# Expert layer of a four-layer conv mixer: when the group sums run, how block sums and weight sums are cut, and where filler matmuls stand

## The chip, the cores and the metric

The kernel runs on one core of one Trainium2 chip. The metric is the device time of one execution in microseconds (us). Five engines work side by side, each with its own queue of instructions in order: TensorE (PE; matmuls, with PEld for its weight loads), VectorE (DVE), ScalarE (ACT), GpSimd (POOL) and SyncE (SP, which issues DMAs). An engine waits for another through semaphores only.

## The reference, cut to what matters

Input x has 8 images of 384 channels and 32x32 pixels, in float32. Four layers follow each other, each as x = x + layer(group_norm(x)), with 32 groups of 12 channels. The change is in layer 1, the experts:

```
x = x + L1(gn(x)):   scores -> top 2 of 4 experts per token
  present[k, e] = any token of the whole batch has e as its k-th choice
  h_e = relu(x . w1_e + b1_e);  y_e = h_e . w2_e + b2_e       (384 -> 384 -> 384)
  out = sum_e y_e * coef_e,  coef_e = sum_k present[k, e] * w_k
```

Where every expert is chosen by some token in both places, all coefficients are one, and the layer is the plain sum of the four experts' outputs. The kernel computes that, keeps the logits, and decides later whether a second pass by token is needed; on these inputs it is not. Behind the layer, group norm needs mean and variance over 12 channels and all pixels of an image.

## The kernel before, in words

Channels lie on partitions, 384 as three tiles (`NC = 3`) of 128. `experts()` (from L1140) loops over the 8 images b and over two halves h of each, 512 pixels a half, cut again into two quarters of 256 columns (`QF`). There are 16 rounds, called here first half and second half of an image. A round has two phases.

*Hidden phase.* For experts 0 to 2 the product w1 . x is made by a fast scheme with 15 block products instead of 18. `dual` (L1284) issues one matmul of 128x256 per product (two records each in the profile) on sums of input blocks, the "forms" (`make_forms`, L1273, 12 sums on GpSimd, a round ahead), and on sums of w1's blocks (`w1sum`, made once by `sum_weights`, L1259). VectorE combines the 15 results out of PSUM (L1304), ScalarE adds bias and rectifies (L1282). The last expert goes the plain way (`classical`, L1310): 3 output tiles by 3 input tiles, nine matmuls of 128x512. These nine are dealt out as fillers, some after the second product of each of the experts 0, 1 and 2 and the rest at the end (L1460 to L1472). In the first round of all, every expert goes the plain way.

*Product phase.* `products` (L1339) multiplies by w2 with the same scheme transposed: 15 products, each of four matmuls of 128x256 (one per expert, eight records), into one PSUM buffer out of five. VectorE adds each result to one to four blocks of the residual r (L1353, L1355). The operands are blocks of the hidden values hs or sums of them, `hs_sum`: eight sums (`HSUMS[:-2]`) before the phase, by GpSimd for each expert as it is ready, and two sums over all experts (128x1024) issued after product 8. Products 0 to 4 read plain blocks; products 5 to 12 read the eight sums in turn, products 13 and 14 the last two. In first halves from image 1 on GpSimd makes those two, else VectorE.

After product i a round runs the jobs listed for i. In first halves from image 1 on these include the steps of `next_layer` (L1383) for the image before: moments of its three channel tiles (`moments2`, L1366, with `centred`, L309, three small VectorE instructions), the sums over groups (`over_groups`, L300, 14 small matmul records into `gn_ps`), `norm2` (L1377, four small VectorE instructions, a power on GpSimd at L332 and a VectorE instruction at L337 which reads it), and four steps that normalise (ScalarE), transpose (VectorE) and store a tile. Other jobs normalise the image's second half, make its forms and fetch the next image's residual. In second halves VectorE adds the layer input to the next image's residual (L1164).

The order of every engine but SP here is the order in which the program writes the instructions (`manual_schedule`). An engine that waits holds up all that is queued behind.

Of the kernel before, what the change touches and what calls it, by code (L numbers as in the profile page):

```python
# [21 lines left out]
NC = C // P  # L22
# [8 lines left out]
E, HID = 4, 384  # L31
# [33 lines left out]
def taps(xp, dy, dx, rows=H, h0=0):  # L65
# [20 lines left out]
WSUMS = (  # L86
    (7, (2, 0), -1, (2, 2)),
    (6, 7, 1, (0, 0)),
    (7, 7, -1, (1, 0)),
    (2, (1, 1), -1, (1, 2)),  # L90
    (3, 2, 1, (0, 1)),
    (2, 2, -1, (2, 1)),
    (10, 6, 1, 3),
    (10, 10, -1, (0, 2)),
# [6 lines left out]
HSUMS = (  # L101
    (4, (1, 1), (2, 1)),
    (0, (0, 1), (2, 1)),
    (10, (2, 0), (2, 1)),
    (3, (1, 1), 10),
    (8, (1, 0), 3),
    (11, (0, 0), 8),
    (6, (0, 1), 10),
    (9, (0, 0), 6),
# [5 lines left out]
R15 = 3  # L115
FORMS = (
    (4, (1, 1), (0, 1), -1),
    (14, 4, (2, 1), 1),
    (13, (2, 0), 14, -1),
    (1, (0, 0), (1, 0), -1),  # L120
    (0, (0, 0), (2, 0), -1),
    (11, (0, 1), (2, 0), -1),
    (3, (2, 1), (0, 1), -1),
    (10, (1, 0), 14, -1),
# [49 lines left out]
def conv_mixer_kernel(ctx: ExitStack, tc: tile.TileContext, a: dict, out: bass.AP):  # L174
    nc = tc.nc
# [234 lines left out]
    with (  # L410
# [38 lines left out]
        with tc.tile_pool(name="cps", bufs=2, space=PSUM, reuse_waits="tile") as cps:  # L449
# [68 lines left out]
            for n, (ct, v, u) in enumerate(groups):  # L518
                if u == 0:

                    o = co.tile([P, B, H, 32], FP, tag="o", name="o")
                w = weights0.pop(n).rearrange("p r t w -> p r (t w)")
                ps = cps.tile([P, 4, 2, B, H], FP, tag="ps", name="ps")
                for cc in range(2):
                    for k in range(3):
                        for e, d, i in product(range(2), repeat=3):
                            r = slice(64 * i, 64 * i + 64)
# [63 lines left out]
    def layers(again, early, xst, pre_pool, pp0, pw):  # L591
# [548 lines left out]
        def experts():  # L1140
# [14 lines left out]
            rs, xns, pls = {}, {}, {}  # L1155
# [97 lines left out]
            def block1(n):  # L1253
                n = {8: (1, 1), 9: (2, 0)}.get(n, n)
                if isinstance(n, tuple):
                    return w1[:, :R15, n[0], n[1] * P : (n[1] + 1) * P]
                return w1sum[:, w1slot[n]]

            def sum_weights():  # L1259
                for o, i, sign, j in [*WSUMS[3:6], *WSUMS[8:10], *WSUMS[:3], *WSUMS[6:8], *WSUMS[10:]]:  # L1260
                    first8 = o == 8 and i != 8
                    nc.gpsimd.tensor_tensor(
                        out=block1(5 if first8 else o), in0=block1(5 if i == 8 else i), in1=block1(j),
                        op=ALU.add if sign > 0 else ALU.subtract,
                    )
# [4 lines left out]
                    return xn[:, n[0], n[1] * QF : (n[1] + 1) * QF]  # L1270
                return forms[:, fslot[n]]

            def make_forms(xn, part=slice(0, len(FORMS))):  # L1273
                for o, i, j, sign in FORMS[part]:
                    i, j = (form_of(v, xn) for v in (i, j))
                    nc.gpsimd.tensor_tensor(
                        out=forms[:, fslot[o]], in0=i, in1=j,
                        op=ALU.add if sign > 0 else ALU.subtract,
                    )
# [55 lines left out]
            def sums(hs, some, s, eng=nc.vector):  # L1335
                for o, i, j in some:
                    eng.tensor_add(rows_of(o, hs, s), rows_of(i, hs, s), rows_of(j, hs, s))  # L1337
# [25 lines left out]
                    for job in jobs.get(i, ()):  # L1363
                        job()

            def moments2(r, b, cts, mv, dq):  # L1366

                for ct in cts:
                    bs = small.tile([P, 2, 6], FP, tag="gn_bs", name="gn_bs")
                    bn_stats_of(bs, r[:, ct, :])  # L1370
                    nc.vector.bn_aggr(mv[:, :, ct], bs.rearrange("p a s -> p (a s)"))
                c = slice(cts[0], cts[-1] + 1)
                centred(
                    dq[:, c], mv[:, 0, c].unsqueeze(2), mv[:, 1, c].unsqueeze(2), ref2[:, c, b : b + 1]
                )
# [7 lines left out]
            def next_layer(b):  # L1383

                r = rs[b]
                mv = small.tile([P, 2, NC], FP, tag="gn_mv", name="gn_mv")
                if b < B - 1:
                    dq = er.tile([P, NC, 2, 1], FP, tag="dq", name="dq")
                    st = er.tile([P, NC, 3], FP, tag="st", name="st")
                    keep_residual(r, b)  # L1390
                    for ct in range(NC):
                        moments2(r, b, (ct,), mv, dq)
                        yield
                    ps = eh.tile([P, NC, 2, 1], FP, tag="sm", name="gn_ps")
                    over_groups(ps, dq, range(NC))
                    yield
                    norm2(ps, b, range(NC), st)
                    yield
                    steps = pass_on_steps(r, b, st[:, :, 0], st[:, :, 1], er)
                    for _ in steps:  # L1400
                        yield
                    return
                dq = er.tile([P, NC, 2, 1], FP, tag="dq", name="dq")
                st = er.tile([P, NC, 3], FP, tag="st", name="st")
                parts = (range(2), range(2, NC))
                cos = (range(1), range(1, NC))
                for i, (cts, co) in enumerate(zip(parts, cos)):
                    if i == len(parts) - 1:
                        keep_residual(r, b)
                    moments2(r, b, cts, mv, dq)  # L1410
                    yield
                    ps = eh.tile([P, NC, 2, 1], FP, tag="sm", name="gn_ps")
                    over_groups(ps, dq, co)
                    yield
                    norm2(ps, b, co, st)
                    yield
                    for ct in co:
                        pass_on(r, b, ct, st[:, :, 0], st[:, :, 1], er)
                        yield
# [26 lines left out]
            for b, h in product(range(B), range(2)):  # L1446
                hs = ew.tile([P, NC, E, HF], FP, tag="hs", name="hs")
                xn = xns[b, h]
                gating = logits(b) if h else iter(())
                if (b, h) == (0, 0):  # L1450
                    for e in (E - 1, *range(E - 1)):
                        for _ in classical(hs, e, range(NC), xn):
                            pass
                        if e == E - 3:
                            for s in (slice(E - 1, E), slice(0, E - 2)):
                                sums(hs, HSUMS[:-2], s)
                    sums(hs, HSUMS[:-2], slice(E - 2, E - 1))
                    sum_weights()
                else:
                    full = classical(hs, E - 1, range(NC), xn)  # L1460
                    for e in range(R15):
                        got = {}
                        dual(hs, e, xn, slice(0, 2), got)
                        next(gating, None)
                        for _ in range(2):
                            next(full)
                        dual(hs, e, xn, slice(2, len(DUAL)), got)
                        if e:
                            sums(hs, HSUMS[:-2], slice(e - 1, e), nc.gpsimd)
                    next(gating, None)  # L1470
                    for _ in full:
                        pass  # L1472
                    for e in range(R15 - 1, E):
                        sums(hs, HSUMS[:-2], slice(e, e + 1), nc.gpsimd)
                if (b, h) == (B - 1, 1):
                    wqpool.close()
                    begin_layer2(B - 1, er)
                jobs = {}

                def at(i, job, *args):  # L1480
                    jobs.setdefault(i, []).append(lambda: job(*args))

                nxt = (b, 1) if h == 0 else (b + 1, 0)
                if h == 0:
                    if passing:
                        for i in (0, 1, 2, 4, 5, 7, 8, 10, 12):
                            at(i, next, passing)
                    at(2, normed, b, 1)
                    half = len(FORMS) // 2
                    at(3, lambda b=b: make_forms(xns[b, 1], slice(0, half)))  # L1490
                    at(6, lambda b=b: make_forms(xns[b, 1], slice(half, len(FORMS))))
                    if b + 1 < B:
                        at(13, fetch_next, b + 1)
                elif b + 1 < B:
                    for i in (0, 1, 3):
                        at(i, next, ahead[b + 1])
                    at(4, normed, b + 1, 0)
                    at(5, lambda b=b: make_forms(xns[b + 1, 0]))
                products(b, h, hs, jobs)
                if h == 1:  # L1500
                    passing = next_layer(b)
# [302 lines left out]
        sums = fe.tile([P, 2, B, 5], FP, name="sums")  # L1804
# [172 lines left out]
        with tc.manual_schedule(engines=ORDERED | {mybir.EngineType.Pool}):  # L1977

            for ct in range(NC):
                o = None  # L1980
                for c in range(8):
# [10 lines left out]
                    if c == 0:  # L1992
# [3 lines left out]
                        o = to.tile([P, B, H, 32], FP, tag="o", name="o")  # L1996
# [562 lines left out]
```

## Time and profile before

| What | Value |
|---|---|
| Median of 3 runs | 3197.67 us (3193.99 to 3200.61) |
| Profiled execution | 3198.98 us, span 3197.1 us |
| Busy: PE, DVE, ACT, POOL | 94%, 60%, 38%, 25% of the span |
| Experts' layer | about 1730 to 2690 us of the span |
| Two rounds (one image) in it | 119.1 to 120.1 us |
| Mean granted TensorE clock | 0.977 of full speed |

The rows that follow name a source line, an engine, the tiles written and read, the shape, a count, and in brackets the engine's idle time before and what ended it. A view by windows gives busy times in a stretch and the granted clock as a share of full speed. Times of rows count from the start of the span.

### The profile page before, as it was taken

How to read it: one execution, taken by the hardware profiler on the slowest of the kernel's cores; microseconds unless marked ns; L12 is line 12 of the kernel's file. 1: busy time of each engine (PE TensorE's matmuls, PEld its weight loads, DVE VectorE, ACT ScalarE, POOL GpSimd, SP SyncE). 2: the span in 40 equal slices, each digit the busy share in tenths (PEclk: the TensorE clock that was granted, in tenths of full speed). 3: DMA queues.
4: the chain of work that ended last, by engine and by line, in shares of the span. 5: the costliest groups of instructions: out<-in, count | busy, mean ns of one | idle time of the engine just before them, and what ended most of it. 6: DMA issues, size and time to landing. Idle time of an engine off the chain costs nothing.

```text
span 3197.1 us, 45217 instructions
## 1 busy us (share of the span) xinstructions
PE 3000.7 (94%) x18280; PEld 1710.7 (54%) x18280; DVE 1907.5 (60%) x3221; ACT 1212.6 (38%) x1446; POOL 807.4 (25%) x1102
## 2 busy tenths in 40 slices
PE   4988999999999999999998999999999999886999
PEld 3765334343434334343433777777777777555543
DVE  6998344444454454444445777777777776447174
ACT  3555453535444453535342122222222222446520
POOL 2432000000000000000003565665665663111400
PEclk9999999999999999999999999999999999988999
DMA  6787011020101111020013012112111114866766
GB/s 220 271 284 288 20 42 62 23 72 33 62 23 60 45 44 58 23 82 23 13 43 142 19 46 59 62 50 54 64 51 52 51 44 137 330 212 232 233 223 190
DMA packets 89107, 323.03 MB, mean 101 GB/s; under 512 B 13608, under 2 KB 16000, under 8 KB 84664
## 3 DMA queue, kind: packets, MB, share of 16 engines
q1 hardware_dynamic: 64936, 251.71, 23.4%
q10 hardware_dynamic: 13776, 35.82, 3.5%
q0 software_dynamic: 10176, 32.51, 3.0%
q8 instruction: 146, 2.39, 0.3%
q14 instruction: 73, 0.60, 0.1%
HBM read 211.66 MB, written 111.68 MB: 101 GB/s over the span
## 4 chain that ended last, share of the span: by engine, by line
PE 73%; DVE 14%; DMA 5%; POOL 3%; issue 3%; ACT 2%; SPq 0%; ACTq 0%; DVEq 0%; POOLq 0%
PE sc L771 15%; PE av L790 14%; PE p L1344 10%; PE p L1295 7%; PE sc L669 7%; PE sc L724 4%; PE ph L1314 4%; PE sc L846 4%; DVE stats L250 2%; DVE y L499 2%; POOL hs_sum L1337 2%; PE ps L1956 2%; DMA w<-in_w 1%; DVE hs L1304 1%; PE po L2370 1%
## 5 line engine op out<-in xcount | busy, mean ns | idle before, releaser
L778 ACT ACTIVATE e<-sc 128x1024 f32<-128x1024 f32 x512 | 483.1, 1029 | 608.2 <-PE sc L771 608.1
L771 PE MATMUL sc<-qT,kT 64*128 64x512 f32 x2048 | 473.9, 602 | 0.0
L790 PE MATMUL av<-e,vT 128*64 128x512 f32 x2048 | 467.7, 598 | 0.0
L771 PEld LDWEIGHTS sc<-qT,kT 64*128 64x128 f32 x2048 | 186.7, 186 | 282.1 <-issue 231.2
L790 PEld LDWEIGHTS av<-e,vT 128*64 128x64 f32 x2048 | 135.5, 136 | 316.5 <-issue 316.5
L1337 POOL TENSOR_TENSOR hs_sum<-hs,hs_sum 128x256 f32<-128x256 f32 (+1 forms) x314 | 266.7, 857 | 19.4
L820 POOL DMA_DIRECT2D att<-att x45 | 23.8, 531 | 979.9 <-DVE att L815 979.9
L806 DVE LOAD_MASK_SELECT sm<-av x64 | 0.9, 14 | 417.0 <-PE av L790 417.0
L669 PE MATMUL sc<-y,pw 128*128 128x512 f32 x576 | 249.3, 594 | 0.0
L528 PE MATMUL ps<-xt,wx 64*64 64x256 f32 x3456 | 196.9, 386 | 36.7 <-DVE xt L466 21.4
L1353 DVE TENSOR_TENSOR r<-r,p 128x256 f32<-128x256 f32 x416 | 154.6, 413 | 106.8 <-PE p L1344 105.2
L808 DVE RECIPROCAL inv<-sm 128x512 f32<-128x512 f32 x64 | 214.6, 3353 | 2.2
L352 ACT ACTIVATE hs<-hs,b 128x512 f32<-128x512 f32 x135 | 89.1, 715 | 322.8 <-DVE hs L1304 322.8
L1337 POOL TENSOR_TENSOR hs_sum<-hs 128x256 f32<-128x256 f32 x180 | 132.8, 766 | 293.0 <-ACT hs L352 293.0
L528 PEld LDWEIGHTS ps<-xt,wx 64*64 64x64 f32 x3456 | 156.3, 137 | 76.2 <-issue 38.3
L669 PEld LDWEIGHTS sc<-y,pw 128*128 128x128 f32 x576 | 108.8, 190 | 140.0 <-issue 138.6
L1114 PE MATMUL ps<-xt,wx 64*64 64x256 f32 (+1 forms) x2912 | 159.1, 377 | 25.4 <-ACT wx L1712 14.4
L1295 PE MATMUL p<-forms,w 128*128 128x256 f32 x630 | 174.5, 387 | 7.4 <-DVE hs_sum L1304 6.6
L1344 PE MATMUL p<-hs_sum,wsum 128*128 128x256 f32 x768 | 173.6, 379 | 0.0
L1304 DVE TENSOR_TENSOR hs<-p,hs_sum 128x256 f32<-128x256 f32 x270 | 113.6, 421 | 83.3 <-PE p L1295 35.6
L1314 PE MATMUL ph<-xn,w 128*128 128x512 f32 x342 | 159.5, 601 | 3.0 <-ACT xn L352 3.0
L1344 PEld LDWEIGHTS p<-hs_sum,wsum 128*128 128x128 f32 x768 | 145.9, 190 | 19.8
(346 smaller groups left out, 4644.4 us busy)
## 6 DMA issues: line engine op xcount, KB each, us to landing
raw<-y SPq DMA_DIRECT2D x72, 512.0 KB
y<-raw SPq DMA_DIRECT2D x24, 1536.0 KB
x<-x SPq DMA_DIRECT2D x23, 608.0 KB
xt<-x SPq DMA_DIRECT2D x23, 608.0 KB
w<-in_w ACTq DMA_DIRECT2D x36, 384.0 KB
xn<-in_x SPq DMA_DIRECT2D x24, 512.0 KB
x<-in_x SPq DMA_DIRECT2D x16, 768.0 KB
z<-z POOLq DMA_DIRECT2D x16, 768.0 KB, 4.3
```

Source lines behind the costliest of these rows:

```text
L528: nc.tensor.matmul(ps[64 * d : 64 * d + 64, 2 * i + e, cc], lhsT=w[r, 12 * cc + 6 * e + 3 * d + k, :], rhs=xt0s[ct][r, 16 * d + 4 * u + 2 ...
L669: nc.tensor.matmul(ps[:, h, :], lhsT=w[:, ct, pair, :], rhs=y[:, ct, h * HF : (h + 1) * HF], start=ct == 0, stop=ct == NC - 1,)
L771: nc.tensor.matmul(sc[:, s, :], lhsT=kTs[b][r, pair, m * P : (m + 1) * P], rhs=qTs[b][r, pair, h * HF : (h + 1) * HF], start=True, stop=True,)
L778: nc.scalar.activation(e, sc, AF.Exp, scale=1.0 if shifted else HD**-0.5)
L790: nc.tensor.matmul(av[64 * s : 64 * s + 64, :], lhsT=vTs[0][:, m, c0 : c0 + 64], rhs=e[:, s, :], start=m == 0, stop=m == N // P - 1,)
L808: nc.vector.reciprocal(inv, sm)
L1114: nc.tensor.matmul(ps[64 * d : 64 * d + 64, 2 * i + e, c % 2, images], lhsT=w[r, d * K7 + k, :], rhs=by_slot(xts[ct])[r, 16 * d + column(c ...
L1295: nc.tensor.matmul(ps[:, :QF], lhsT=block1(PRODUCTS[n][0])[:, e], rhs=form_of(n, xn), start=True, stop=True,)
L1314: nc.tensor.matmul(ph, lhsT=w1[:, e, ct, dc * P : (dc + 1) * P], rhs=xn[:, ct, :], start=ct == 0, stop=ct == NC - 1,)
L1337: eng.tensor_add(rows_of(o, hs, s), rows_of(i, hs, s), rows_of(j, hs, s))
L1344: nc.tensor.matmul(ps[:, :QF], lhsT=block(w)[:, e], rhs=rows_of(x, hs, e), start=e == 0, stop=e == E - 1,)
L1353: nc.vector.tensor_tensor(out=o, in0=o, in1=ps[:, :QF], op=op)
```

## The change

Five edits, all in `experts()`:

1. The three centrings of an image (one per channel tile, behind each tile's moments) become one over all three tiles, as a step of its own after the moments. The group sums follow after product 6 (product 4 before), `norm2` after 7 (5), and the four passing steps after 9, 10, 12 and 14 (7, 8, 10 and 12).
2. The eight block sums of experts 2 and 3 are made together, one instruction of 512 columns for both, instead of one of 256 columns for each.
3. Of the 13 sums of w1's blocks, the first eight (in the order of the list) are issued before the first round's products, and five after product 4, behind the forms.
4. Fillers: three after the second product of expert 0, then two, two, and two at the end (before: two, two, two, three).
5. In first halves all twelve forms are issued after product 3 (before: six after 3, six after 6). The fetch of the next residual moves from product 13 to 14.

```diff
-            def sum_weights():
-                for o, i, sign, j in [*WSUMS[3:6], *WSUMS[8:10], *WSUMS[:3], *WSUMS[6:8], *WSUMS[10:]]:
+            def sum_weights(some):
+                for o, i, sign, j in some:
...
-            def moments2(r, b, cts, mv, dq):
+            def moments2(r, b, cts, mv):
...
                     nc.vector.bn_aggr(mv[:, :, ct], bs.rearrange("p a s -> p (a s)"))
+
+            def centred2(dq, mv, b, cts):
                 c = slice(cts[0], cts[-1] + 1)
                 centred(
                     dq[:, c], mv[:, 0, c].unsqueeze(2), mv[:, 1, c].unsqueeze(2), ref2[:, c, b : b + 1]
...
                     for ct in range(NC):
-                        moments2(r, b, (ct,), mv, dq)
+                        moments2(r, b, (ct,), mv)
                         yield
+                    centred2(dq, mv, b, range(NC))
+                    yield
                     ps = eh.tile([P, NC, 2, 1], FP, tag="sm", name="gn_ps")
...
-                    sum_weights()
+                    sum_weights(WSUMS[:8])
...
-                        for _ in range(2):
+                        for _ in range(2 + (e == 0)):
                             next(full)
...
-                    for e in range(R15 - 1, E):
-                        sums(hs, HSUMS[:-2], slice(e, e + 1), nc.gpsimd)
+                    sums(hs, HSUMS[:-2], slice(R15 - 1, E), nc.gpsimd)
...
                     if passing:
-                        for i in (0, 1, 2, 4, 5, 7, 8, 10, 12):
+                        for i in (0, 1, 2, 3, 6, 7, 9, 10, 12, 14):
                             at(i, next, passing)
                     at(2, normed, b, 1)
-                    half = len(FORMS) // 2
-                    at(3, lambda b=b: make_forms(xns[b, 1], slice(0, half)))
-                    at(6, lambda b=b: make_forms(xns[b, 1], slice(half, len(FORMS))))
+                    at(3, lambda b=b: make_forms(xns[b, 1]))
+                    if b == 0:
+                        at(4, sum_weights, WSUMS[8:])
                     if b + 1 < B:
-                        at(13, fetch_next, b + 1)
+                        at(14, fetch_next, b + 1)
```

More of the change, by code (lines that the diff above doesn't have):

```diff
@@ L1271, in form_of, with make_forms @@
                 return forms[:, fslot[n]]
-            def make_forms(xn, part=slice(0, len(FORMS))):
-                for o, i, j, sign in FORMS[part]:
+            def make_forms(xn):
+                for o, i, j, sign in FORMS:
                     i, j = (form_of(v, xn) for v in (i, j))
@@ L1409, in next_layer @@
                         keep_residual(r, b)
-                    moments2(r, b, cts, mv, dq)
+                    moments2(r, b, cts, mv)
+                    centred2(dq, mv, b, cts)
                     yield
```

## The prediction

> **What bounds the kernel now.** I read the engine rows of the page first, then the windows over the experts' stage (1780 to 2700 us), then TensorE's waits in it, and last the timeline of one image.
>
> ```profile
> PE 3000.7 (94%) x18280; PEld 1710.7 (54%) x18280; DVE 1907.5 (60%) x3221; ACT 1212.6 (38%) x1446; POOL 807.4 (25%) x1102
> ...
> 1840.00:1900.00 60.00, 56.17 (x233) 44.69 (x232) 44.09 (x107) 11.61 (x21) 39.59 (x53) 0.95 0.13 27
> 1900.00:1960.00 60.00, 58.28 (x265) 45.69 (x265) 46.74 (x105) 16.02 (x25) 34.75 (x44) 1.00 0.25 84
> ...
> PE gn_ps L304 <- DVE dq L313: 34.7, 16, 8.2
> PE p L1344 <- POOL hs_sum L1337: 8.7, 7, 1.3
> ```
>
> (Windows: length, then busy us and records of PE, PEld, DVE, ACT and POOL, the granted clock, DMA share, GB/s. Waits: us in total, times, longest.) TensorE sets the pace, in this stage too (56 to 58 of every 60 us). Its two stalls there are the ones the change touches: the group sums wait for VectorE's centring, and products wait for GpSimd's block sums. The window with a group sum in it has a granted clock of 0.95, the other 1.00. The timeline of image 1's first half shows why:
>
> ```profile
> 1890.39 0.28 PE L304 MATMUL gn_ps<-dq,gmatA 128*128 128x2 f32 x2
> 1891.09 0.83 PE L304 MATMUL gn_ps<-dq,gmatA 128*128 128x2 f32 x6 [0.42 <-DVE dq L313]
> 1894.86 1.44 PE L304 MATMUL gn_ps<-dq,gmatA 128*128 128x2 f32 x6 [2.94 <-DVE dq L313]
> 1896.16 5.76 PE L1344 MATMUL p<-hs_sum,w 128*128 128x256 f32 x16
> ```
>
> And three windows of 2 us across it:
>
> ```profile
> 1894.00:1896.00 2.00, 1.14 (x6) 1.14 (x6) 1.97 (x6) 0.00 (x0) 1.92 (x4) 0.50 0.00 0
> 1898.00:1900.00 2.00, 2.00 (x6) 1.63 (x5) 0.04 (x1) 0.00 (x0) 1.94 (x3) 0.50 0.00 0
> 1902.00:1904.00 2.00, 2.00 (x11) 1.77 (x10) 1.66 (x4) 1.13 (x1) 2.00 (x4) 1.00 0.00 0
> ```
>
> After the wait the clock is 0.50, and 16 matmul records take 5.76 us. At full clock 24 take 5.34, so a record is 0.2157 us and a product (8 records) 1.726. GpSimd's queue in the same half is the other thing to see:
>
> ```profile
> 1895.55 0.73 POOL L1276 TENSOR_TENSOR forms<-xn 128x256 f32<-128x256 f32 x1
> ...
> 1901.26 0.86 POOL L332 TENSOR_TENSOR st<-fm_b,mhalf 128x3 f32<-128x3 f32 x1 [1.32 <-DVE st L326]
> 1902.09 0.73 POOL L1276 TENSOR_TENSOR forms<-xn 128x256 f32<-128x256 f32 x1
> ...
> 1906.21 4.82 POOL L1337 TENSOR_TENSOR hs_sum<-hs,hs_sum 128x1024 f32<-128x1024 f32 x2
> ...
> 1902.15 0.68 DVE L337 SCALAR_TENSOR_TENSOR st<-st 128x3 f32<-128x3 f32 x1 [0.90 <-POOL st L332]
> ```
>
> Six forms, the power (L332), six forms, then two wide sums that products 13 and 14 read. It ends at 1911.0; product 13 starts only at 1912.1 (the next half at 1915.57 less two products), so GpSimd is just hidden today.
>
> **What today's stalls cost.** From the group sum's start to the next half's first matmul: 25.2, 25.0, 24.4, 25.0, 24.4, 25.0, 24.4 us for images 1 to 7, mean 24.8. Ten products are 17.26 and 14 small matmuls 0.9. So 6.6 us are lost per image, wait and slow clock together. In second halves of images 0 to 6 the first 46 records (9.92 us) start at 1945.81 and the 47th at 1957.15: 1.42 lost, 9.9 in all.
>
> **Group sums after product 6, one centring.** Now three centrings of three instructions each sit among the moments (1.3 us each: 1886.03 to 1887.37 is one). Taking them out brings the third moment's end from 1893.2 to 1890.2, with products 0.3 us earlier (below); two evictions (0.9) give 1891.1, and one centring 1.3 to 2.7 (up to two GpSimd sums of 1.27 in its way): 1892.4 to 1893.8. Product 6 ends at 1893.5. The stall goes, or 0.3 is left.
>
> **Two experts' sums together.** Per half 16 GpSimd instructions of 256 columns (0.72 us) become 8 of 512. No 512-wide sum of these blocks is in the trace. Bounds: the line through 256 columns (0.72) and 1024 (2.37) gives 1.27; w2's sums of 512 columns (L1248) run 1.27 to 1.44, the upper end beside busy VectorE. I take 1.27, since in this stretch VectorE mostly reads one operand from SBUF; 8 of them, paced as the present ones are (8 in 5.97), come to 10.4, against 11.95 now. They begin later, since the last expert's rectification (ScalarE, to 1884.13) must be done: 1884.2 to 1894.6, a gain of 0.95. The first sum is there at 1885.5, for all experts that remain, where now the last expert's is ninth. Product 5 wants it after 1891, so second halves lose their 1.42 wait: -9.9.
>
> **The forms undivided: what is late next.** All twelve now stand ahead of the power, and the wide sums behind it. Replaying image 1 on its own times: forms 1894.6 + 8.5 (4.4 + 4.1 now) = 1903.1, power to 1903.95, wide sums to 1906.35 and 1908.8. VectorE has the power's inputs by 1898.5 and then stands still, with the evictions of products 8 to 12 behind it, until its L337. That row is 0.68 now beside a form that ends with it (1902.82), 0.16 for the last image, where GpSimd is idle. So it waits for whatever GpSimd began: here a 2.4 us sum. Bounds 0.16 and 2.4; I take 2.4, as all seven images show the whole remainder waited. VectorE is free at 1906.35, product 8's bank at 1907.15. With five banks, product 13 starts then; 12 ended at 1904.8. The half ends at 1907.2 + 3.45 = 1910.65 instead of 1915.57. Group sum to end falls from 24.8 in the mean to 20.3: -4.5.
>
> The Trainium skill, page "SBUF — State Buffer", section "Who interferes with whom", says that a VectorE instruction with two SBUF inputs and a GpSimd instruction that reads SBUF exclude each other for a whole instruction. L337 (0.68 beside 0.16) agrees; by that rule the 2.4 is right, and were it 0.16 instead, the sum would be some 12 us lower.
>
> **Fillers 3, 2, 2 and 2.** One 128x512 matmul pair (0.863) moves ahead of the first expert's third product, which delays VectorE's whole chain by as much, because it waits for TensorE at each expert's start (1.2 to 2.0 us): +0.86 per first half, so -3.64 net, x7 = -25.5. At the end one filler fewer: the first product's third expert wants its rectified block 0.86 sooner (1945.81 for 1946.29), +0.53 in second halves: x8 = +4.2. In first halves it vanishes in the new wait.
>
> **Second half's start, images 1 to 7.** VectorE comes late: from 1906.35, the evictions of products 8 to 14 and three transposes (1.99 each, each behind ScalarE's 1.24) end at 1918.7, as 1906.35 + 0.75 + 0.4 + 1.4 + 2.0 + 0.75 + 0.4 + 0.1 + 2.0 + 1.4 + 1.1 + 2.0 gives. TensorE, begun at 1910.65, waits 0.65 for a bank at its second product, spends 1.4 on logits and 2.6 on three fillers, and at the eighth product waits 0.8 and a little after: +1.65, x7 = +11.6. With VectorE free 2.2 us sooner it would be 0; with GpSimd 1 us slower about 2.6.
>
> **Weights' sums in two parts.** GpSimd's total to 1780 is the same, and the next reader is at 1795. VectorE's last five sums take 0.91 beside forms, the three before 1.16 beside weights' sums; the forms now come first, so about 1.0 is gained before product 5 of image 0: -1.0. Hidden by that 15 us: the five moved sums. SP's fetch of the next residual moves one product later, behind the last read of the old one (about 1915.5 instead of 1913.5), wanted at 1948.5: nothing.
>
> **The clock.** The new gap before product 13 is 2.4 us in one piece. 2.9 after 0.4 halves the clock in all seven images, for 3.3 or 6.8 us; 1.4 in second halves never. The halving stretches begin at 3.4 us steps, and the least idle time inside such a step that halved it is 2.3 (image 3). So perhaps one image in three is hit, at 1.7 us: bounds 0 and 24 (3.4 each), taken +3. The Trainium skill, "TensorE: Matmul & The Clock Gate", section "Why this matters for your kernels", asks for no idle gap over about 3 us; by it the term is 0 and the sum 3 us lower, which no run here shows yet.
>
> Sum: -25.5 - 9.9 + 4.2 + 11.6 - 1.0 + 3 = -17.6. The profiled execution (3198.98, span 3197.1) lies 1.3 above the median of the runs, 3197.67; taken from the median: 3180.
>
> **Rivals.**
> - L337 slips in ahead of the wide sum. Product 13 then starts at 1906.4, the half ends at 1910.5, and second halves start unhindered: 3167. Against it: 0.68 in seven of seven.
> - GpSimd is no bound at all, the stalls just vanish: 46 + 10 - 8 + 1 = 49 less, 3149. It needs the queue 2.4 us shorter than any row makes it.
> - Slower: the 512-wide sums. Everything in first halves is pinned to GpSimd's queue, so each us there costs 7. Eight at 1.27 are in the sum; the gain is gone at 17.6/7/8 = 0.31 more (1.58), a clear loss from 1.7. Two present sums take 1.50 (then 3191); at 1.9 it is 3213. Against it: no 512-column row above 1.45.
> - The clock falls for 6.8 us in every image: 3201, the same within what is measurable.
> - The change doesn't do what it says: the group sums still wait at product 6. Up to 2.4 us of that would be hidden by the wait at 13; beyond, 3195.
>
> **How the numbers follow.** Chances: as summed 0.47 (own range 3170 to 3190), L337 early 0.12, no new bound 0.08, GpSimd slower 0.19, clock 0.08, group sums still waiting 0.06. About 0.2% (6.4 us) is what a measurement can tell. Faster 0.67, same 0.14, slower 0.19. Range 3154 to 3204: from near the free case to the slower case's edge.
>
> **What would show it.** Right: group sums wait under 0.5 us; no POOL wait in second halves; L337 at about 2.4 us; a gap before product 13, put down to VectorE's evictions or hs_sum; 512-wide sums at 1.27. Wrong: L337 at 0.16 or 0.7, full clock with products unbroken, or 512-wide rows over 1.5.

## The result, and the profile after

| | before | after |
|---|---|---|
| median | 3196.01 us (4 runs, 3193.99 to 3200.61) | 3170.97 us (4 runs, 3165.36 to 3177.68) |
| profiled execution | 3198.98 us, span 3197.1 | 3177.68 us, span 3175.9 |

The ratio of the times is 0.9921, with a 95% interval of 0.9896 to 0.9945: faster by 0.8%, or 25 us between the medians. The profiled execution of after is the slowest of its four, so that the two profiles lie only 21.3 us apart. The time forecast was 3180.

The page's row of engines and the two windows that were shown of before, now of after (in the second kind of line: length, busy us and records of PE, PEld, DVE, ACT and POOL, granted clock, DMA share, GB/s):

```profile
PE 3001.4 (95%) x18280; PEld 1696.7 (53%) x18280; DVE 1912.0 (60%) x3179; ACT 1213.5 (38%) x1446; POOL 787.4 (25%) x982
```
```profile
1840.00:1900.00 60.00, 59.11 (x259) 47.31 (x258) 45.18 (x109) 11.76 (x21) 39.29 (x46) 1.00 0.15 32
1900.00:1960.00 60.00, 57.63 (x257) 43.07 (x256) 47.84 (x99) 15.97 (x25) 35.96 (x40) 1.00 0.25 84
```

TensorE's records are as many as before. VectorE has 42 fewer (14 centrings of three instructions each), GpSimd 120 fewer (15 rounds of eight sums each). The window with image 1's group sums went from 56.17 to 59.11 us of busy TensorE, and from a clock of 0.95 to 1.00. The next window lost: 58.28 to 57.63. Both matter below.

TensorE's waits from 1720 to 2700 us of after, which is the experts' layer and a little on both sides (total us, times, longest):

```profile
PE gn_ps L304 <- DVE dq L313: 11.1, 2, 8.2
PE p L1344 <- DVE r L1353: 8.7, 7, 1.3
...
PE p L1344 <- ACT hs L352: 6.2, 15, 0.4
```

The group sums' wait for the centring fell from 34.7 us in 16 places to 11.1 in two, and those two lie outside the seven first halves. The wait for `hs_sum` (8.7 us in seven) is gone. A new one stands in their place, again seven times, 1.3 us at most: product 13 waits for an eviction (L1353). And the first product of 15 rounds waits 0.4 us for ScalarE's rectification.

Image 1's first half in after, TensorE:

```profile
1883.11 4.58 PE L1344 MATMUL p<-hs,w 128*128 128x256 f32 x20 [0.42 <-ACT hs L352]
...
1894.43 1.62 PE L304 MATMUL gn_ps<-dq,gmatA 128*128 128x2 f32 x14
1895.91 5.43 PE L1344 MATMUL p<-hs_sum,wsum 128*128 128x256 f32 x24
...
1902.90 3.62 PE L1344 MATMUL p<-hs_sum,wsum 128*128 128x256 f32 x16
1907.78 1.97 PE L1344 MATMUL p<-hs_sum,w 128*128 128x256 f32 x8 [1.26 <-DVE r L1353]
```

GpSimd and VectorE in the same stretch:

```profile
1884.98 3.75 POOL L1337 TENSOR_TENSOR hs_sum<-hs 128x512 f32<-128x512 f32 x3 [3.82 <-ACT hs L1324]
1888.81 6.54 POOL L1337 TENSOR_TENSOR hs_sum<-hs,hs_sum 128x512 f32<-128x512 f32 x5
1895.31 0.72 POOL L1276 TENSOR_TENSOR forms<-xn 128x256 f32<-128x256 f32 x1
...
1903.77 0.86 POOL L332 TENSOR_TENSOR st<-fm_b,mhalf 128x3 f32<-128x3 f32 x1
1904.60 4.80 POOL L1337 TENSOR_TENSOR hs_sum<-hs,hs_sum 128x1024 f32<-128x1024 f32 x2
```
```profile
1904.67 2.30 DVE L337 SCALAR_TENSOR_TENSOR st<-st 128x3 f32<-128x3 f32 x1 [4.95 <-POOL st L332]
1906.89 2.59 DVE L1353 TENSOR_TENSOR r<-r,p 128x256 f32<-128x256 f32 x7
...
1916.83 1.98 DVE L1014 STREAM_TRANSPOSE x<-xn 128x1024 f32<-128x1024 f32 x1
```

Read it as a relay. GpSimd works without a break from 1884.98 to 1909.40: sums, twelve forms, the power, the wide sums. VectorE idles 4.95 us until the power is there, and its answer, L337, works on three columns but takes 2.30 us; GpSimd's first wide sum starts 0.07 us ahead of it, and `last_dve` below shows that this is the reason. Seven evictions wait behind L337, and product 13 waits for the first two of them, which are product 8's, because products 8 to 12 hold all five banks.

To compare whole images, I cut the layer at the first matmul record of each phase (L1295 or L1314 for a hidden phase, L1344 for a product phase). The layer runs here from the first matmul of image 0 to the first matmul of the next layer.

| mean us | before | after |
|---|---|---|
| image 0, first half: hidden phase | 32.81 | 33.21 |
| image 0, first half: product phase | 33.22 | 30.48 |
| first halves, images 1 to 7: hidden phase | 28.66 | 28.61 |
| first halves, images 1 to 7: product phase | 33.28 | 29.64 |
| second halves, images 1 to 7: hidden phase | 30.27 | 31.69 |
| second halves, images 0 to 6: product phase | 27.41 | 26.58 |
| second half, image 7: product phase | 27.28 | 27.97 |
| the experts' layer | 960.97 | 937.53 |

The layer is 23.4 us shorter between the profiles. The rest of the span, which the change does not touch, is 2.2 us longer (2236.1 to 2238.4): 3.1 longer ahead of the layer and 0.9 shorter behind it.

### The profile page after: what moved, and what is told of

It reads as the page before. It is cut to its first block, busy times and chain, and to the rows that moved or that the text cites. A ratio compares the mean times of both kernels' runs of the same rounds, so it can differ in the third digit from the quotient of the medians.

```text
span 3175.9 us, 45058 instructions
## 1 busy us (share of the span) xinstructions
PE 3001.4 (95%) x18280; PEld 1696.7 (53%) x18280; DVE 1912.0 (60%) x3179; ACT 1213.5 (38%) x1446; POOL 787.4 (25%) x982
## 4 chain that ended last, share of the span: by engine, by line
PE 74%; DVE 14%; DMA 5%; issue 3%; POOL 2%; ACT 1%; SPq 0%; ACTq 0%; DVEq 0%; POOLq 0%
PE sc L771 15%; PE av L790 14%; PE p L1344 10%; PE p L1295 8%; PE sc L669 7%; PE sc L724 4%; PE sc L846 4%; PE ph L1314 4%; DVE stats L250 3%; DVE y L499 2%; DVE hs L1304 2%; PE po L2374 1%; PE po L2377 1%; PE po L2385 1%; DVE xt L466 1%
## 5 line engine op out<-in xcount | busy, mean ns | idle before, releaser
L1337 POOL TENSOR_TENSOR hs_sum<-hs,hs_sum 128x256 f32<-128x256 f32 (+1 forms) x239 | 247.1, 1042 | 14.7
L1337 POOL TENSOR_TENSOR hs_sum<-hs 128x256 f32<-128x256 f32 (+1 forms) x135 | 132.9, 1013 | 271.6 <-ACT hs L352 214.3
L1353 DVE TENSOR_TENSOR r<-r,p 128x256 f32<-128x256 f32 x416 | 152.9, 412 | 67.9 <-PE p L1344 64.7
L1295 PE MATMUL p<-forms,w 128*128 128x256 f32 x630 | 178.5, 391 | 8.4 <-DVE hs_sum L1304 6.3
L1344 PE MATMUL p<-hs_sum,wsum 128*128 128x256 f32 x768 | 174.2, 380 | 0.0
L1314 PE MATMUL ph<-xn,w 128*128 128x512 f32 x342 | 159.9, 602 | 3.0 <-ACT xn L352 3.0
L1344 PEld LDWEIGHTS p<-hs_sum,wsum 128*128 128x128 f32 x768 | 145.0, 190 | 19.9
```

Of the source, the lines that this page charges most:

```text
L1295: nc.tensor.matmul(ps[:, :QF], lhsT=block1(PRODUCTS[n][0])[:, e], rhs=form_of(n, xn), start=True, stop=True,)
L1314: nc.tensor.matmul(ph, lhsT=w1[:, e, ct, dc * P : (dc + 1) * P], rhs=xn[:, ct, :], start=ct == 0, stop=ct == NC - 1,)
L1344: nc.tensor.matmul(ps[:, :QF], lhsT=block(w)[:, e], rhs=rows_of(x, hs, e), start=e == 0, stop=e == E - 1,)
```

## The experiments

My theory, as in the prediction: after the change a first half's end is pinned to GpSimd's queue, through the power, L337 and the wide sums, and second halves start late because VectorE waits out a wide sum in L337. The rivals: VectorE's own load sets both, or the group sums and the centring do, whatever GpSimd's order is. All diffs are against after, except that of `edit1_alone`.

### Forms in two parts again, later: split7 and split8

The forms are the only large work ahead of the power that is wanted later than it. Six of them move behind it; `split7` issues them after product 7, still ahead of the wide sums, `split8` after product 8, behind the wide sums. The diff is that of `split8`; `split7` has 7 in its last line.

```diff
-            def make_forms(xn):
-                for o, i, j, sign in FORMS:
+            def make_forms(xn, part=slice(0, len(FORMS))):
+                for o, i, j, sign in FORMS[part]:
...
-                    at(3, lambda b=b: make_forms(xns[b, 1]))
+                    half = len(FORMS) // 2
+                    at(3, lambda b=b: make_forms(xns[b, 1], slice(0, half)))
+                    at(8, lambda b=b: make_forms(xns[b, 1], slice(half, len(FORMS))))
```

> The changed kernel, but the twelve forms cut again: six after product 3, six after product 7, behind the power. Theory G (GpSimd's queue sets product 13, and VectorE stands behind the power and the wide sum that follows it): the power starts at about 1899.8 in image 1's times instead of 1903.8, L337 runs beside a form (0.7 us, not 2.3), VectorE is free some 5 us sooner. The wide sums end where they end now (1909.4), so the product phase of first halves stays near 29.5 us (29.65 now); the hidden phase of second halves falls from 31.69 to 30.25. Together 10 us less over seven images. Theory V (VectorE's own work after the later group sums is what is late): no change in either phase.

> The changed kernel, but six forms after product 3 and six after product 8, behind the two wide sums. Theory G: power at 1899.8, wide sums from 1900.6 to 1905.4, before product 12 ends (1906.5); L337 still waits out a wide sum (2.3 us) but ends at 1902.9, so product 8's bank is free in time. No gap before product 13: first halves' product phase 28.3 us (29.65 now), second halves' hidden phase 30.25 (31.69 now), together about 19 us less. Theory V: neither changes, since VectorE has the same instructions.

Measured: `split7` 3164.77 us, ratio 0.9899 (0.9872 to 0.9926); `split8` 3154.61, 0.9873 (0.9850 to 0.9895). In phases (first halves' product phase; second halves' hidden phase; layer): 29.61, 30.24, 926.62 and 28.15, 30.28, 918.63, where after has 29.64, 31.69 and 937.53. GpSimd's queue in image 1 of `split8`:

```profile
1900.48 0.86 POOL L332 TENSOR_TENSOR st<-fm_b,mhalf 128x3 f32<-128x3 f32 x1
1901.31 4.80 POOL L1337 TENSOR_TENSOR hs_sum<-hs,hs_sum 128x1024 f32<-128x1024 f32 x2
1906.07 0.73 POOL L1276 TENSOR_TENSOR forms<-xn 128x256 f32<-128x256 f32 x1
```

The power's row stands 3.3 us earlier than in after, and so do the wide sums, though image 1's product phase begins 0.84 us later in this run (1882.50 for 1881.66): within the phase they are 4.1 us earlier. VectorE's L337 in `split8`, and all seven of it in `split7` (minimum, median and maximum in ns, first and last start):

```profile
1901.37 2.31 DVE L337 SCALAR_TENSOR_TENSOR st<-st 128x3 f32<-128x3 f32 x1 [0.83 <-POOL st L332]
```
```profile
L337 DVE SCALAR_TENSOR_TENSOR st<-st x7: 678/681/689, 1900.5 to 2590.7; 128x3 f32<-128x3 f32 x7
```

Behind a wide sum L337 takes 2.31, behind a form 0.68. What follows: the two losses have two causes that can be set apart. In `split7` the wide sums end as late as in after, and the product phase keeps its 29.6; VectorE is free early, and the second half starts unhindered. In `split8` the wide sums come early as well, and both losses go, though L337 is as long as in after: early enough, its 2.3 us cost nothing. The theory that GpSimd's queue pins product 13 holds; that VectorE's own load does falls.

### Wide sums on VectorE: last_dve

```diff
-                        sums(hs, HSUMS[-2:], slice(0, E), nc.gpsimd if begun_all else nc.vector)
+                        sums(hs, HSUMS[-2:], slice(0, E), nc.vector)
```

> The changed kernel, but the two wide sums of first halves on VectorE, behind product 8's eviction, so that no wide GpSimd sum follows the power. If L337's 2.3 us is the wait for a running GpSimd instruction (G), it is 0.16 to 0.2 here; if it is L337's own cost or the power's signal, it stays 2.3. By G the gap before product 13 falls from 1.3 to about 0.4 us (its sum is ready at 1906.9), first halves' product phase to 28.8, while VectorE, which pays 2.4 us for the sums, is 0.4 later at the second half: hidden phase 31.7 to 32.1. Together 3 to 6 us less.

Measured: 3170.37 us (2 runs), ratio 0.9920 (0.9891 to 0.9948). All seven of L337:

```profile
L337 DVE SCALAR_TENSOR_TENSOR st<-st x7: 161/163/164, 1900.5 to 2599.9; 128x3 f32<-128x3 f32 x7
```

With GpSimd idle behind the power, the same instruction takes 0.163 us, so 2.14 of its 2.30 are waiting. This is no wait for a semaphore: the power, which L337 does wait for by semaphore, ends at 1904.63 in after, and L337's row begins at 1904.67. So one engine can hold up another here without any semaphore. The Trainium skill, page "SBUF — State Buffer", section "Who interferes with whom", says that a VectorE instruction with two SBUF inputs and a GpSimd instruction that reads SBUF lock each other out for a whole instruction. The three values agree: 2.30 beside a wide sum, 0.68 beside a form, 0.16 beside nothing. The product phase came to 28.53, near the 28.8 expected. The hidden phase did not: 32.80, where 31.7 to 32.1 was expected, because the wide sums are now VectorE's work (2.47 us in image 1): product 13 starts in time, but the second half's second product waits 1.3 us for an eviction (L1353) in all seven images. The layer came to 937.25, no gain (-0.3) where 3 to 6 us were expected. Moving work off the engine that waits only helps if the taker has time just then.

### Two more forms on GpSimd: pool_more

The last two forms are computed a second time into the same places, for the same values.

```diff
+            def again_forms(xn):
+                for o, i, j, sign in FORMS[-2:]:
...
                     at(3, lambda b=b: make_forms(xns[b, 1]))
+                    if b > 0:
+                        at(3, lambda b=b: again_forms(xns[b, 1]))
```

> The changed kernel with two of the twelve forms computed twice in first halves from image 1 on (the same values again), which lengthens GpSimd's queue ahead of the power by 1.4 us. Theory G: all of it shows: first halves' product phase 29.65 to 31.0, the gap before product 13 from 1.3 to 2.7 us, second halves' hidden phase 31.69 to about 33.1, together some 19 us more. Theory V: nothing, as VectorE has the same work. The clock: a gap of 2.7 us in one piece halves it in some images (one to three of seven) if 2.3 us idle inside a 3.4 us step is what decides; in none if it takes about 3 us.

Measured: 3185.59 us, ratio 0.9971 (0.9960 to 0.9982). In images 1, 3, 5 and 7 the product phase is 30.95, 1.31 more for 1.4 us of added GpSimd work, and the gap before product 13 is 2.55 to 2.58: as expected of a queue that is the bound. In images 2, 4 and 6 it is 32.63. The windows of image 2 show why (columns as above):

```profile
2025.00:2027.00 2.00, 0.05 (x1) 0.08 (x1) 1.90 (x4) 0.82 (x1) 1.92 (x2) 1.00 0.00 0
2027.00:2029.00 2.00, 2.00 (x7) 1.65 (x8) 2.00 (x6) 0.42 (x1) 1.57 (x1) 0.68 0.00 0
2029.00:2031.00 2.00, 2.00 (x6) 1.55 (x5) 2.00 (x3) 0.43 (x1) 0.40 (x2) 0.50 0.00 0
```

After the gap the granted clock is 0.50 for 3.4 us. But the layer grew by only 9.1 us (946.61), and I had the hidden phase wrong: it stayed at 31.68 where 33.1 was expected. TensorE is itself later by what GpSimd is later, so VectorE's lateness against it does not grow. After a halved clock it is even 30.23, so 1.45 of the 1.69 us that halving costs come back in the next phase. The profiled execution is the fastest of the eight; how many images were halved in the others is not on record.

### The group sums alone: edit1_alone

On before, only the first edit: one centring, group sums after product 6, and with them the residual's fetch after 14.

```diff
-            def moments2(r, b, cts, mv, dq):
+            def moments2(r, b, cts, mv):
...
+            def centred2(dq, mv, b, cts):
...
+                    centred2(dq, mv, b, range(NC))
+                    yield
...
-                        for i in (0, 1, 2, 4, 5, 7, 8, 10, 12):
+                        for i in (0, 1, 2, 3, 6, 7, 9, 10, 12, 14):
...
-                        at(13, fetch_next, b + 1)
+                        at(14, fetch_next, b + 1)
```

> The kernel before with one edit: group sums after product 6 with one centring (and the passing steps and the fetch at their later products); block sums, weights' sums, fillers and forms as before. By G the stall at the group sums goes, and GpSimd's queue takes over: sums to 1895.6 in image 1's times, all forms to 1904.1 (the second six are now ahead of the power), power to 1904.9, wide sum and L337 to 1907.3, product 13 from 1908.1. First halves' product phase 29.8 us (33.3 before), second halves' hidden phase 32.5 (30.25), since VectorE is late and only two fillers cover it, second halves' product phase 27.4 as before. Together 8 to 9 us less than before. Rival (the stall was what mattered, and little takes its place): product phase 28.5, hidden phase 30.25, 33 us less.

Measured: 3187.05 us, ratio 0.9972 (0.9962 to 0.9982); the layer is 951.68, 9.3 us less. The size is about the one expected; its make-up is so in three images of seven. TensorE's waits and two windows of 3.4 us in image 2:

```profile
PE p L1344 <- DVE r L1353: 14.5, 7, 2.1
...
PE p L1344 <- POOL hs_sum L1337: 8.7, 7, 1.3
```
```profile
2024.20:2027.60 3.40, 1.28 (x7) 0.83 (x6) 3.09 (x4) 0.86 (x1) 3.32 (x3) 1.00 0.00 0
2027.60:2031.00 3.40, 3.40 (x9) 2.69 (x10) 3.40 (x7) 0.38 (x1) 1.52 (x1) 0.51 0.00 0
```

The group sums wait no more, but product 13 waits up to 2.1 us instead, and in images 2, 3, 5 and 6 that halves the clock: product phases of 31.46 there against 29.78 in images 1, 4 and 7. Second halves keep their wait for `hs_sum`, and their hidden phase is 32.53 (30.83 after a halved clock). Both phases together take 62.3 us with and without the halving, so here it costs nothing in all: the slower products give VectorE the time to catch up. So this edit alone turns one stall into the next, and the other edits are needed to shrink that one.

### Block sums apart again: sums_apart

```diff
-                    sums(hs, HSUMS[:-2], slice(R15 - 1, E), nc.gpsimd)
+                    for e in range(R15 - 1, E):
+                        sums(hs, HSUMS[:-2], slice(e, e + 1), nc.gpsimd)
```

> The changed kernel with the block sums of experts 2 and 3 apart again (eight of 256 columns each). Second halves wait for GpSimd again: product phase 27.4 us (26.58 now). First halves: GpSimd's queue 0.9 longer, product phase 30.5 (29.64 now). Hidden phases unchanged. Together 11 to 13 us more than the changed kernel. If the merged sums gave nothing, both phases stay.

Measured: 3191.6 us (one run, so that the profiles alone are compared); the layer is 957.50, 20.0 us more than after, where 11 to 13 were expected.

```profile
PE p L1344 <- DVE r L1353: 16.0, 7, 2.3
PE p L1344 <- POOL hs_sum L1337: 10.0, 7, 1.5
```

Without the merged sums GpSimd's forms begin 14.7 us after the product phase instead of 13.65. The gap before product 13 grows by that 1.0, from 1.26 to 2.28, and in images 2 to 7 the clock is halved: product phases of 30.67 in image 1 and 32.32 in the others. Second halves have their wait for `hs_sum` back: 28.28 against 26.58, more than the 27.4 expected. The likely reason is that the 3, 2, 2 and 2 fillers stay: `edit1_alone`, with the sums apart and 2, 2, 2 and 3, has 27.41, and the difference is one filler's 0.86. So the merged sums are worth 1.0 us in a first half and 1.7 in a second. They also keep the gap below the point where the clock reacts, but that is worth little: of the 1.66 us by which a halved product phase is longer 1.43 come back in the hidden phase behind it (30.24 for 31.67). What is left is some 1.4 us in the whole layer.

### Fillers 2, 2, 2 and 3: fillers_back

```diff
-                        for _ in range(2 + (e == 0)):
+                        for _ in range(2):
```

> The changed kernel with fillers 2, 2, 2 and 3 as before. The wait of the first product for ScalarE (0.6 us) goes: second halves' product phase 25.95 us (26.58 now). First halves' product phase, pinned to GpSimd's queue, 28.8 (29.64). Second halves' hidden phase: one filler fewer covers VectorE's late start, 32.5 (31.69). Together 3 to 6 us less than the changed kernel: the fillers' edit by itself cost time. Rival (the filler ahead covers more than it costs): hidden phase 33 or more, together 3 us more or worse.

Measured: 3169.35 us, ratio 0.9912 (0.9897 to 0.9927); the layer is 931.70, 5.8 less than after. The profile's waits:

```profile
PE p L1344 <- DVE r L1353: 7.3, 7, 1.1
...
PE p L1295 <- DVE hs L1304: 6.2, 7, 0.9
```

The wait of the first product for ScalarE is gone, and with it 0.68 in second halves (25.90) and 0.89 in first (28.75). Most of the latter comes back as a later second half (32.52 against 31.69). The filler edit by itself costs time in this kernel. This rests on the two profiles, whose phases agree to 0.03 us from image to image; the medians of the whole runs lie only 1.6 us apart, less than the runs of one kernel differ.

### What these runs point to: best

Fillers 2, 2, 2 and 3; the forms at 3 and 8 from image 1 on, where the wide sums are GpSimd's, and together at 3 in image 0, since `split8` lost 1.9 us there (product phase 32.64 against 30.78 in `split7`).

```diff
...
-                        for _ in range(2 + (e == 0)):
+                        for _ in range(2):
...
+                    half = len(FORMS) // 2
+                    if b == 0:
+                        at(3, lambda b=b: make_forms(xns[b, 1]))
+                    else:
+                        at(3, lambda b=b: make_forms(xns[b, 1], slice(0, half)))
+                        at(8, lambda b=b: make_forms(xns[b, 1], slice(half, len(FORMS))))
```

> The changed kernel with six forms behind the two wide sums from image 1 on (all after product 3 in image 0) and fillers 2, 2, 2 and 3. Against the run with the same order of forms but fillers 3, 2, 2, 2 (3154.6): the first product's wait of 0.63 us goes in 15 rounds (9.4 us), image 0's product phase falls from 32.6 to 30.5 us, and second halves' hidden phase grows by up to 0.5 us where VectorE is late. First halves' product phase 27.5, second halves' 25.95. Together 7 to 12 us less: 3143 to 3148.

Measured: 3140.51 us (5 runs, 3138.47 to 3144.35), ratio 0.9823 (0.9810 to 0.9836) to before, a little under the range expected. The phases are 27.46, 30.27 and 25.90, the layer 907.30. TensorE's largest waits from 1720 to 2700 us, and the windows:

```profile
PE gn_ps L304 <- DVE dq L313: 11.1, 2, 8.2
PE p L1295 <- DVE hs_sum L1304: 6.2, 15, 0.4
...
PE p L1344 <- DVE r L1355: 3.1, 1, 3.1
```
```profile
1840.00:1900.00 60.00, 59.53 (x262) 47.99 (x261) 45.27 (x110) 11.60 (x21) 40.12 (x47) 1.00 0.14 30
1900.00:1960.00 60.00, 59.51 (x273) 47.14 (x272) 51.66 (x106) 15.81 (x25) 39.36 (x43) 1.00 0.25 84
```

No wait that comes seven times is among them any more, and TensorE is busy 59.5 of every 60 us at full clock.

## Why the prediction was right, point by point

| term | predicted | measured, profile against profile |
|---|---|---|
| first halves, images 1 to 7 | -3.64 x7 = -25.5 | -3.65 x7 = -25.5 |
| second halves' product phase | -1.42 + 0.53 = -0.89, x7 = -6.2 | -0.83 x7 = -5.8 |
| last product phase (image 7) | +0.53 | +0.68 |
| second half's start | +1.65 x7 = +11.6 | +1.42 x7 = +9.9 |
| image 0, first half | -1.0 | -2.74 + 0.40 = -2.3 |
| clock | +3 | 0 |
| sum | -17.6 | -23.4 in the layer |

The measured column adds up to -23.0; the rest is rounding and phases that are not listed.

- **The relay came as replayed.** L337 was put at 2.4 and took 2.30; the eight merged sums take 10.3 us for 10.4 reckoned; product 13 starts 26.1 us into the product phase (1907.78 for a phase that begins at 1881.66) where 26.3 was reckoned (1907.15 and the filler's 0.86, in a phase from 1881.75). Undoing single links confirms each: `split7` frees VectorE alone, `split8` also GpSimd, `last_dve` removes L337's wait, and `pool_more` adds 1.4 us to GpSimd and gets 1.31.
- **The second half's start** was reckoned from VectorE's late transposes. That is shown: in `split7` and `split8`, where VectorE is done earlier, it is 30.24 and 30.28, the value of before. The forecast's 2.6 for a GpSimd that is 1 us slower does not hold: in `pool_more` GpSimd is 1.4 us slower, and the phase stays at 31.68.
- **The clock was the term that was mis-sized.** The gap before product 13 was reckoned at 2.4 us and is 1.26; the granted clock stays 1.00 around it in all seven images. Product 13 starts when forecast; product 12 ends 1.7 us later than forecast (1906.52 for 1904.8). The 14 small group-sum records take 1.48 us (1894.43 to 1895.91) where I had 0.9, the first product's wait for ScalarE (0.42) was not counted into this path, and the products, reckoned 0.3 us earlier than in before, are not earlier. I had also left the filler's 0.86 out of the gap, which by the forecast's own times is 3.2. Time that TensorE spent ahead of a pinned product cost nothing and made the gap harmless: that the clock stayed full was luck. The price was wrong as well: a halved step costs an image 0 to 0.25 us in all (`edit1_alone`, `pool_more`, `sums_apart`), not 1.7 or 3.4, as the next phase gives most of it back.
- **Image 0** gained more. Its wait before product 5 fell from 4.36 to 2.62 us, and the 16 slow records behind it from 6.42 to 5.41: two gains, of which I had priced part of the first only. The edit of the weights' sums was not run alone. In `edit1_alone`, without it, the phase is 33.17, and it lies between 29.83 and 30.95 in the kernels that have it with undivided forms. In `split7`, which has it with divided forms, it is 30.78, so the undivided forms are not the reason. The weights' sums are the likely cause; the runs do not show them by themselves.
- **The filler edit** was priced right in second halves' products (0.53 for 0.68 when undone) and first halves (0.86 for 0.89). Its two terms together, 0.86 x7 and 0.53 x8, put the edit down as a loss of some 10 us; taken out again it gives back only 5.8, because 0.83 of the 0.89 in each first half comes back as a later second half.
- **The rivals.** L337 slipping in ahead of the wide sum happened in no image of any run that leaves the sum behind the power. 512-wide sums are paced at 1.25 (3.75 for 3) and 1.31 (6.54 for 5), far from the 1.58 at which the gain would be gone. (At 7 us for each us the rival's 1.50 and 1.9 give 3193 and 3215, not 3191 and 3213; nothing rests on these.) The clock rival did not come true in this kernel: `edit1_alone`, `sums_apart` and `pool_more` show that the clock does fall at gaps little longer, and that it costs far less than the rival's 24 us.

Of the difference between the medians, 25.0 us, the layer's 23.4 explains nearly all. What stays open: runs of one and the same kernel spread over 4 to 13 us, and the rest of the span differs by 2.2 between the two profiles. In the ten profiles the layer starts between 1729.0 and 1733.8 us, though the code ahead of it is the same in all, so such a difference is nothing that the change made; no run here traces it to a cause.

## What to carry to other kernels

When a change removes a stall, replay the queue that becomes the next bound instruction by instruction, at its rows' durations, before you price the gain: here that gave the new wait's place and the start of product 13 to 0.2 us. In an in-order queue put first what someone waits for soonest: six forms that were wanted in the next round stood ahead of sums wanted at once, and moving them behind, an edit of a few lines, was worth 19 us in the layer. A stall or a slow clock is priced on the whole path: what one phase loses the next gave back almost whole here. And a small instruction that answers another engine's result pays for whatever that engine starts next, so either have it early or put short work behind the result.

## What was not expected of the hardware

**The clock reacts to less than the 2.3 us of idle time that the prediction had read in before.** In `edit1_alone` the slow stretches start at 2027.65, 2147.11, 2382.63 and 2502.10: 35, 69 and 35 steps of 3.41 us apart. All four follow a gap of 2.04 to 2.12 us that lies wholly inside the step before. In images 1, 4 and 7 a gap as long (2.08 in image 1) falls on a boundary of two steps, and the clock stays at 1.00. In `pool_more` gaps of 2.55 to 2.58 halve it in three images and not in four, where the larger piece is 1.95 at most; in `sums_apart` 1.93 inside a step in image 1 did not, 2.15 to 2.26 inside one in the six others did. So on these runs the limit for a gap between large matmuls lies near 2.0 us of idle time within one step, and a halved step costs 1.7 us in its own phase. The Trainium skill, page "TensorE: Matmul & The Clock Gate", section "Why this matters for your kernels", asks to avoid idle gaps above about 3 us; these runs show less than that to be enough, and the measurement decides.

Before itself has less still, which the prediction's 2.3 overlooked. In its images 2, 4 and 6 the slow stretch follows a step in which TensorE is idle 1.24 to 1.41 us. In image 2 that is the step up to 2012.99:

```profile
2009.58:2012.99 3.41, 2.04 (x14) 1.73 (x12) 3.31 (x8) 0.00 (x0) 3.25 (x6) 1.00 0.00 0
```

Eight of its records are small group sums (128x2), unlike in the gaps above. Whether these count for less than their busy time says is not shown by any run here.

**GpSimd's next instruction wins over the one it released.** L337 waits for the power, and the instruction that follows the power on GpSimd starts 0.07 us before it in after (1904.60 and 1904.67). In all seven images of `after`, `split7`, `split8` and `best` L337 shows the wait, its length being that of the instruction GpSimd had begun.
